# Denominators of linear attention inverted between two block transpositions, squares made by ScalarE, and a third buffer of key sums

## The chip, the cores and the metric

The kernel runs on one NeuronCore of a Trainium2 chip. The metric is the device time of one execution in microseconds. A NeuronCore has engines that run their own instruction queues side by side and wait for one another by semaphores: TensorE (PE in the profile, its weight loads PEld), VectorE (DVE), ScalarE (ACT), GpSimd (POOL) and SyncE (SP), which here issues the DMAs. Each engine executes its queue in order. Data lies in SBUF (128 partitions) or in PSUM, which has eight banks of 128 x 512 fp32 and takes what TensorE writes.

## The reference

Two images of 512 channels and 64 x 64 positions pass through four layers, each of the form x + layer(groupnorm(x)). The change concerns the fourth, an attention with random features (8 heads of 64 channels, 256 features):

```python
def _favor_softmax_features(data, proj, is_query):
    d = data.shape[-1]
    m = proj.shape[0]
    ratio = m ** (-0.5)
    normalizer = d ** (-0.25)
    data_dash = jnp.einsum('bhnd,md->bhnm', data * normalizer, proj)
    diag = 0.5 * jnp.sum((data * normalizer) ** 2, axis=-1, keepdims=True)
    if is_query:
        stab = jnp.max(data_dash, axis=-1, keepdims=True)
    else:
        stab = jnp.max(data_dash, axis=(-2, -1), keepdims=True)
    return ratio * (jnp.exp(data_dash - diag - stab) + EPS)
...
q = split_heads(t @ Wq)
k = split_heads(t @ Wk)
v = split_heads(t @ Wv)
qp = _favor_softmax_features(q, proj, is_query=True)
kp = _favor_softmax_features(k, proj, is_query=False)
context = jnp.einsum('bhnm,bhnd->bhmd', kp, v)
k_sum = jnp.sum(kp, axis=-2)
denom = jnp.einsum('bhnm,bhm->bhn', qp, k_sum)
out = jnp.einsum('bhnm,bhmd->bhnd', qp, context) / denom[..., None]
out = out.transpose(0, 2, 1, 3).reshape(B, N, C) @ Wo
```

Each token has one denominator a head.

## The kernel before

One image lies whole in SBUF as 4 chunks of 128 channels by 4096 positions (`X`, called `big0` or `big1` in the profile); the other image's space is lent out until the next image is loaded. A layer's work goes in 8 blocks of 512 positions (`blk`), and a block in 4 chunks of 128 channels, two heads each (`cc`). Matrix products are fp32; one product of 128 x 128 by 128 x 512 shows as two records of TensorE.

The fourth layer first goes over all blocks for the keys (`key_context`), which leaves the context `ctxm`, the key sums `ksum` and the small terms of EPS (`ends`). Then comes the stage of the queries, class `Queries`, `run` (L1800 on). For each block there are three generators, which `in_turn` steps one after the other until all are done:

- `prepare(blk)` (L1836), through `projected_squares` (L1544): for each chunk four matmuls make the query projection in a PSUM bank named `mm` (by `project`, L134), ScalarE copies it with its bias to `k` (L1554), and POOL squares it into `sq` (L1556).
- `score(blk)` (L1841): for each chunk, `features` multiplies `k` by the random projection in two halves and two heads (L1939, four `mm` banks) and ScalarE takes exponentials into `qf`, or into a lent part of an image, `big` (L1942). VectorE sums the squares (L1852) and takes the maxima over features (L1855) while it transposes 32 x 32 blocks. At the end of a block three small transposing matmuls (L1863) bring these together, ScalarE and VectorE make from them one factor for each token and head, `half`, which goes to DRAM (`lost`, L1873).
- `attend(blk)` (L1877): the factors come back from DRAM, repeated over 64 partitions for each head (`lost_all`, `fetch`, L1887). For each chunk POOL adds the two feature halves after weighing one by the ratio of the key sums (`qf_sum`, L1892 and L1894, for two heads); TensorE makes the numerator `psO` (L1906) and the denominator `psD` (L1910), the latter with the key sum repeated over 64 columns, so that all 64 partitions of a head hold the same row; VectorE adds the small term to the denominator (L1913), inverts it (L1914), adds the small term to the numerator (L1915) and multiplies the two into `k` (L1917). After four chunks the output projection follows (L1924), with the sum into `X` (L1927) and the store (L1928).

`attend(blk)`, `prepare(blk + 1)` (from block 1 to 6) and `score(blk + 1)` are stepped in turn, so a block's attention, the next block's features and the projection of the block after it are written interleaved. Block 0 has no projection beside it (that of block 1 was made with the first scores), the last block has neither. On top of that a scheduler reorders instructions within each engine's queue, by its own estimate of when they are ready; the orders named here are those of the compiled program.

PSUM has eight banks here: five for `mm` (shared by projections, features, score transpositions and output projections), two for `psO`, one for `psD`. `qf_sum` has two buffers, that is one chunk's pair; `lost_all` two; `sq` four. In the first three blocks the features of chunks 2 and 3 lie in the same lent place each time, so the next block's exponentials for it wait until the POOL sums have read it.

After the first image's stage, the second image's first layer begins: its weights are loaded into the space of the first image as that comes free, and its statistics are made within the last blocks (L965 to L978).

The parts that matter most, with their lines:

Of the kernel before, what the change touches and what calls it, by code (L numbers as in the profile page):

```python
# [9 lines left out]
F32 = mybir.dt.float32  # L10
I32 = mybir.dt.int32
AF = mybir.ActivationFunctionType
ALU = mybir.AluOpType
# [3 lines left out]
P = 128  # L17
# [4 lines left out]
TB = 512  # L22
# [20 lines left out]
def bcast(ap, axis, n):  # L43

    a = ap.unsqueeze(axis)
    shape = list(a.shape)
    shape[axis] = n
    return a.to_broadcast(shape)
# [10 lines left out]
class General:  # L59
# [130 lines left out]
    def layer0(self, X, Y, sp_scale, tokT, d):  # L190
        tc, nc, vec = self.tc, self.nc, self.vec
        with tc.tile_pool(name="l0", bufs=1) as sp:
# [7 lines left out]
            with tc.tile_pool(name="l0b", bufs=2) as wp, \  # L200
                    tc.tile_pool(name="l0s", bufs=2, space=PSUM) as pps, \
                    tc.tile_pool(name="l0m", bufs=3, space=PSUM) as pp, \
                    tc.tile_pool(name="l0o", bufs=1, space=PSUM) as ppo:
                taps = wp.tile([18, 9, P], F32, name="taps", bufs=1)
                nc.sync.dma_start(taps, d["taps"])
                steps = []
                for cc in range(KC):
                    steps += self.local_chunk(X, Y, cc, xs, nmean, rstd, sp_scale, tokT, taps, d,
                                              wp, pps, pp, ppo)
                in_turn(steps[0][0]())  # L210
                for i, (_, attend) in enumerate(steps):
                    ahead = [steps[i + 1][0]()] if i + 1 < len(steps) else []
                    in_turn(attend(), *ahead)
# [63 lines left out]
    def local_chunk(self, X, Y, cc, xs, nmean, rstd, sp_scale, tokT, taps, d, wp, pps, pp, ppo):  # L277
# [137 lines left out]
        def attend(blk):  # L415
# [48 lines left out]
            nc.vector.tensor_tensor(Y[:, cc, blk * TB:(blk + 1) * TB], acc, psO, ALU.add)  # L464

        return [(lambda b=b: prepare(b), lambda b=b: attend(b)) for b in range(NB)]


# [465 lines left out]
class Net(General):  # L934
# [606 lines left out]
                    queries.run(Y, dst, fp, pp, ppo, ppd, after_keys)  # L1541
        self.ahead.close()

    def projected_squares(self, X, w, bias, blk, out, sqs, wp, pp, made=()):  # L1544

        nc = self.nc
        for cc in range(KC):
            if made:
                ps = made[cc]
            else:  # L1550
                ps = pp.tile([P, TB], F32, name="mm")
                self.project(ps, w[:, :, cc * P:(cc + 1) * P], X, blk)
            k = out[:, cc, :]
            nc.scalar.activation(k, ps, AF.Identity, bias=bias[:, cc:cc + 1])  # L1554
            sq = wp.tile([P, TB], F32, name="sq", bufs=4)
            nc.gpsimd.tensor_tensor(sq, k, k, ALU.mult)  # L1556
            sqs.append(sq)
            yield

# [31 lines left out]
    def key_context(self, X, Y, d, queries, kp, wp, pp):  # L1591
# [54 lines left out]
        def contract(blk):  # L1646
            ks, ed, va = made.pop(blk)
            kf = {}
            for cc in range(KC):
# [31 lines left out]
                yield  # L1681

        in_turn(prepare(0))
        for blk in range(NB - 1):
            in_turn(contract(blk), prepare(blk + 1))
# [85 lines left out]
class Queries:  # L1771
# [64 lines left out]
    def prepare(self, blk, pp):  # L1836
        qs, sqs = self.wp.tile([P, KC, TB], F32, name="k"), []
        self.made[blk] = qs, sqs
        yield from self.net.projected_squares(self.X, self.wq, self.bq, blk, qs, sqs, self.wp, pp)

    def score(self, blk, fp, pp):  # L1841

        nc = self.nc
        qs, sqs = self.made.pop(blk)
        lost = self.yp.tile([2, KC, TB], F32, name="lost")
        fs = []
        self.scored[blk] = qs, lost, fs
        tops = fp.tile([P, 2, KC, 2, 16], F32, name="top_cols")
        sums = fp.tile([P, KC, 16], F32, name="sq_cols")
        for cc in range(KC):  # L1850
            fs.append(self.features(qs[:, cc], self.place(blk, cc, fp), pp))
            nc.vector.tensor_reduce(sums[:, cc], sqs[cc].rearrange("p (b i) -> p b i", i=32), AX.X,  # L1852
                                    ALU.add, apply_transpose=True)
            for h, f in enumerate(fs[cc]):
                nc.vector.tensor_reduce(tops[:, h, cc], f.rearrange("p j (b i) -> p j b i", i=32),  # L1855
                                        AX.X, ALU.max, apply_transpose=True)
            yield
        top = fp.tile([P, 2, KC, 16], F32, name="top_col")
        nc.vector.tensor_tensor(top, tops[:, :, :, 0], tops[:, :, :, 1], ALU.max)
        yield  # L1860
        ps = pp.tile([P, TB], F32, name="mm")
        for i, t in enumerate((sums, top[:, 0], top[:, 1])):
            nc.tensor.transpose(ps[:P // 2, i * P:(i + 1) * P], t.rearrange("p c b -> p (c b)"),  # L1863
                                self.net.ident)
        half = fp.tile([P // 2, 2, 32], F32, name="half")
        nc.vector.tensor_reduce(half, ps[:P // 2, :P].rearrange("p (h c i) -> p h i c", h=2, i=32),
                                AX.X, ALU.add)
        nc.scalar.activation(half, half, AF.Exp, scale=0.5 * HD ** -0.5)
        top = fp.tile([P // 2, 2, 32], F32, name="tops")
        nc.vector.tensor_reduce(top, ps[:P // 2, P:3 * P].rearrange(  # L1870
            "p (h c i) -> p h i c", h=2, i=32), AX.X, ALU.max)
        nc.vector.tensor_tensor(half, half, top, ALU.mult)
        nc.sync.dma_start(lost.rearrange("h c (b i) -> (c b) h i", i=32), half)  # L1873
        nc.vector.tensor_tensor(self.low, self.low, top, ALU.min)
        nc.vector.tensor_tensor(self.high, self.high, half, ALU.max)
        yield

    def attend(self, blk, ratio, dst, fp, pp, ppo, ppd):
        nc, X, ends, ctxm, ksum = self.nc, self.X, self.ends, self.ctxm, self.ksum
        qs, lost, fs = self.scored.pop(blk)  # L1880
        ends_of = {}

        def fetch(cc):

            ends_of[cc] = t = fp.tile([P, TB], F32, name="lost_all", bufs=2)
            for h in range(2):
                nc.sync.dma_start(t[h * HD:(h + 1) * HD, :], bcast(lost[h, cc], 0, HD))  # L1887

        def added(cc):
            ts = [fp.tile([P, TB], F32, name="qf_sum", bufs=2) for h in range(2)]  # L1890
            for h, t in enumerate(ts):
                nc.gpsimd.tensor_scalar(t, fs[cc][h][:, 1], ratio[:, 2 * cc + h:2 * cc + h + 1],  # L1892
                                        None, ALU.mult)
                nc.gpsimd.tensor_tensor(t, t, fs[cc][h][:, 0], ALU.add)  # L1894
            return ts

        for cc in range(2):
            fetch(cc)
        for cc in range(KC):
            sums = added(cc)  # L1900
            psD = ppd.tile([P, TB], F32, name="psD")
            psO = ppo.tile([P, TB], F32, name="psO")
            heads = [slice(h * HD, (h + 1) * HD) for h in range(2)]
            for j in range(2):
                for h, ch in enumerate(heads):
                    nc.tensor.matmul(psO[ch, :], ctxm[:, j, 2 * cc + h, :], fs[cc][h][:, j],  # L1906
                                     start=(j == 0), stop=(j == 1))
            for h, ch in enumerate(heads):
                g = 2 * cc + h
                nc.tensor.matmul(psD[ch, :], ksum[:, 0, g:g + 1].to_broadcast([P, HD]),  # L1910
                                 sums[h], start=True, stop=True)
            t = ends_of.pop(cc)
            nc.vector.scalar_tensor_tensor(psD, t, ends[:, 1, cc:cc + 1], psD, ALU.mult, ALU.add)  # L1913
            nc.vector.reciprocal(psD, psD)  # L1914
            nc.vector.scalar_tensor_tensor(t, t, ends[:, 0, cc:cc + 1], psO, ALU.mult, ALU.add)  # L1915

            nc.vector.tensor_tensor(qs[:, cc, :], t, psD, ALU.mult)  # L1917
            if cc + 2 < KC:
                fetch(cc + 2)
            yield  # L1920
        for oc in range(KC):
            ps = pp.tile([P, TB], F32, name="mm")
            for kc in range(KC):
                nc.tensor.matmul(ps, self.wo[:, kc, oc * P:(oc + 1) * P], qs[:, kc, :],  # L1924
                                 start=(kc == 0), stop=(kc == KC - 1))
            xx = X[:, oc, blk * TB:(blk + 1) * TB]
            nc.vector.tensor_tensor(xx, xx, ps, ALU.add)  # L1927
            nc.sync.dma_start(dst[:, oc, blk * TB:(blk + 1) * TB], xx)  # L1928
            yield
# [936 lines left out]
```

## Time and profile before

| what | value |
|---|---|
| median of 3 runs | 5015.74 us (5015.45 to 5020.18) |
| the profiled execution | 5015.88 us, its span 5014.0 us |
| mean granted TensorE clock | 0.984 |
| queries of the first image | about 2100 to 2522 us |
| queries of the second image | about 4588 us to the end |
| L1914, reciprocals | 64, 3362 ns each, 215.1 us |
| L1556, squares by POOL, median | 1.04 us |
| L1554, copy with bias by ScalarE | 0.69 us |

The page gives each engine's busy time over the whole span; the views by stretch, by waiting instruction and in order of time give the same for one stage. An idle time in brackets stands before the instruction that ends it, with the instruction that released it. Line numbers are those of the kernel before; the tail of a group such as `x64` is its count.

### The profile page before, as it was taken

Reading aid. Unit: us, or ns where it says so; the run is one execution under the profiler, and the core shown is the slowest. Engines: PE = TensorE matmul, PEld = TensorE weight load, DVE = VectorE, ACT = ScalarE, POOL = GpSimd, SP = SyncE. Lnnn points to the kernel's source line nnn. Section 1 sums busy time; section 2 is a strip of 40 time slices with the busy share of each in tenths; the row PEclk is TensorE's granted clock in tenths of the full one; section 3 lists DMA queues with packets and bytes.
Section 4 is the critical chain, followed back from the end, with each engine's and each line's share of the span. In section 5 each row is a group of like instructions: output and inputs, shape, how many; then the busy total and the mean of one; then the engine's idle time right before and its main releaser. Section 6 shows DMA issues by size and latency. Waiting matters only on the chain. (4 is left out here: it accounts for less than half of the span.)

```text
span 5014.0 us, 48290 instructions
## 1 busy us (share of the span) xinstructions
PE 4771.4 (95%) x16883; PEld 1971.8 (39%) x16883; DVE 3074.1 (61%) x3958; ACT 1816.8 (36%) x3477; POOL 1859.1 (37%) x1220
## 2 busy tenths in 40 slices
PE   7999998999999999999999999989999999999998
PEld 3433332554334444433343333335543344444333
DVE  4367776744679533477732777767446794335776
ACT  1256664244323233322112566642443242333221
POOL 0046665501320145554500466654014101554554
PEclk9999999999999999999999999999999999999999
DMA  3035555500000000211120455555000000000111
GB/s 154 1 103 155 155 156 164 160 19 10 1 17 0 1 1 1 72 55 44 58 74 2 126 154 157 151 159 150 12 10 1 17 1 1 1 1 24 43 45 43
DMA packets 129440, 313.29 MB, mean 62 GB/s; under 512 B 23394, under 2 KB 36194, under 8 KB 127652
## 3 DMA queue, kind: packets, MB, share of 16 engines
q1 hardware_dynamic: 129188, 310.12, 21.6%
q8 instruction: 135, 2.21, 0.2%
q14 instruction: 117, 0.96, 0.1%
HBM read 260.73 MB, written 49.31 MB: 62 GB/s over the span
## 5 line engine op out<-in xcount | busy, mean ns | idle before, releaser
L134 PE MATMUL mm<-big,w 128*128 128x512 f32 x2496 | 1164.9, 610 | 16.3 <-DVE big L2448 11.5
L134 PEld LDWEIGHTS mm<-big,w 128*128 128x128 f32 x2496 | 452.6, 191 | 698.3 <-issue 557.2
L2669 POOL TENSOR_TENSOR late<-late,big 128x1024 f32<-128x1024 f32 x194 | 458.5, 2363 | 223.4 <-DVE big L2664 185.4
L2489 DVE TENSOR_TENSOR prods<-qs,big 128x1024 f32<-128x1024 f32 (+1 forms) x200 | 332.2, 1686 | 60.1 <-PE tap L2527 49.1
L1669 POOL TENSOR_TENSOR big<-big 128x512 f32<-128x512 f32 x224 | 277.8, 1273 | 219.4 <-ACT big L1660 219.4
L2664 DVE TENSOR_TENSOR big<-big,mm 128x512 f32<-128x512 f32 x388 | 253.1, 681 | 114.9 <-ACT mm L2656 107.0
L1660 ACT ACTIVATE big<-mm,ed 128x256 f32<-128x256 f32 x512 | 193.5, 489 | 233.1 <-DVE top L1656 200.7
L2656 ACT COPY mm<-big 128x512 f32<-128x512 f32 x432 | 245.8, 597 | 60.4 <-DMA big<-rows 25.1
L2574 POOL TENSOR_TENSOR late<-late 128x512 f32<-128x512 f32 x84 | 105.3, 1275 | 410.5 <-ACT late L2559 393.9
L2669 POOL TENSOR_TENSOR late<-late,tap 128x1024 f32<-128x1024 f32 x94 | 222.1, 2363 | 94.5 <-DVE tap L2664 80.1
L1472 POOL TENSOR_TENSOR wq<-prob 128x512 f32<-128x512 f32 x48 | 71.6, 1515 | 487.9 <-ACT prob L1469 476.5
L1656 DVE TENSOR_REDUCE top<-mm 128x1 f32<-128x512 f32 x256 | 159.0, 684 | 148.1 <-PE mm L1587 148.1
L1924 PE MATMUL mm<-k,w 128*128 128x512 f32 x512 | 235.1, 602 | 12.4 <-DVE k L1917 7.5
L134 PE MATMUL mm<-big,wq 128*128 128x512 f32 x512 | 236.7, 608 | 2.7 <-ACT off_t L1243 2.7
L1215 PE MATMUL mm<-big,wo 128*128 128x512 f32 x512 | 238.1, 611 | 0.0
L1382 PE MATMUL acc<-big,diag 128*128 128x512 f32 x512 | 228.7, 604 | 9.8 <-ACT diag L1387 4.6
L1634 PE MATMUL mm<-w,big 128*128 128x512 f32 x512 | 234.5, 601 | 0.0
L973 POOL TENSOR_TENSOR group_stats<-group_stats,cst 128x1 f32<-128x1 f32 (+1 forms) x20 | 20.2, 1025 | 566.4 <-DVE group_stats L972 510.2
L2527 PE MATMUL tap<-prods,cst 128*32 128x512 f32 x1152 | 189.6, 620 | 29.2 <-ACT late L2538 26.5
L1914 DVE RECIPROCAL psD<-psD 128x512 f32<-128x512 f32 x64 | 215.1, 3362 | 1.9
L134 PE MATMUL mm<-big,big 128*128 128x512 f32 x464 | 201.7, 594 | 0.5 <-DVE b_sr L1011 0.5
L1469 ACT ACTIVATE prob<-mm 128x512 f32<-128x512 f32 x256 | 133.2, 603 | 171.4 <-PE mm L1466 171.1
(428 smaller groups left out, 8114.1 us busy)
## 6 DMA issues: line engine op xcount, KB each, us to landing
big<-rows SPq DMA_DIRECT2D x432, 256.0 KB
tap<-rows SPq DMA_DIRECT2D x208, 256.0 KB
yd<-late SPq DMA_DIRECT2D x32, 512.0 KB
lost_all<-lost SPq DMA_DIRECT2D x128, 128.0 KB
out<-big SPq DMA_DIRECT2D x64, 256.0 KB
big<-in_W_kv SPq DMA_DIRECT2D x8, 1024.0 KB
rows<-late SPq DMA_DIRECT2D x64, 128.0 KB
big<-in_x SPq DMA_DIRECT2D x32, 256.0 KB
```

The costliest lines, as they stand in the source:

```text
L134: self.nc.tensor.matmul(ps, w[:, kc, :], X[:, kc, blk * TB:(blk + 1) * TB], start=(kc == 0), stop=(kc == KC - 1))
L1215: nc.tensor.matmul(ps, w[:, kc, oc * P:(oc + 1) * P], att[:, kc, :], start=(kc == 0), stop=(kc == KC - 1))
L1382: nc.tensor.matmul(accs[b], dg, src[:, b * TB:(b + 1) * TB], start=(j == 0), stop=(j == 6))
L1634: nc.tensor.matmul(ps, X[:, kc, lo:lo + P], wv[:, kc, :], start=(kc == 0), stop=(kc == KC - 1))
L1660: nc.scalar.activation(f[:, t, :], pS[h][i][:, t % 2, :], AF.Exp, bias=ed[:, t, 2 * cc + h:2 * cc + h + 1])
L1669: nc.gpsimd.tensor_tensor(a, a, part, ALU.add)
L1914: nc.vector.reciprocal(psD, psD)
L1924: nc.tensor.matmul(ps, self.wo[:, kc, oc * P:(oc + 1) * P], qs[:, kc, :], start=(kc == 0), stop=(kc == KC - 1))
L2489: self.nc.vector.tensor_tensor(self.pair(u, k)[:, :n].rearrange("p k (y x) -> p k y x", x=W), bcast(qs.rearrange("p (y x) -> p y x", x=W), ...
L2656: nc.scalar.copy(ps, part)
L2664: nc.vector.tensor_tensor(part.rearrange("p (y x) -> p y x", x=W), self.vx[:, y:y + self.UY // 2, dx:dx + W], ps.rearrange("p (y x) -> p y ...
L2669: nc.gpsimd.tensor_tensor(out, out, t, ALU.add)
```

## The change

Three edits in the fourth layer's queries. For blocks 1 to 7 the squares are made by ScalarE, from the PSUM bank with the bias, instead of by POOL from the copy. `qf_sum` gets a third buffer; for the space, a small tile for maxima (`tops`, 64 x 64) is put into the tile of the squares' sums, `sq_cols`. The denominators, equal in the partitions of a head, are no longer inverted as 128 x 512: VectorE transposes each 32 x 32 block within the bank, inverts one column of each block (128 x 16), and transposes back while it repeats that column 32 times; the result goes to the second buffer of the chunk's key sums, whose matmul is done, and L1917 reads it there.

```diff
-    def projected_squares(self, X, w, bias, blk, out, sqs, wp, pp, made=()):
+    def projected_squares(self, X, w, bias, blk, out, sqs, wp, pp, made=(),
+                          by_act=False):
...
             nc.scalar.activation(k, ps, AF.Identity, bias=bias[:, cc:cc + 1])
             sq = wp.tile([P, TB], F32, name="sq", bufs=4)
-            nc.gpsimd.tensor_tensor(sq, k, k, ALU.mult)
+            if by_act:
+                nc.scalar.activation(sq, ps, AF.Square, bias=bias[:, cc:cc + 1])
+            else:
+                nc.gpsimd.tensor_tensor(sq, k, k, ALU.mult)
...
-        yield from self.net.projected_squares(self.X, self.wq, self.bq, blk, qs, sqs, self.wp, pp)
+        yield from self.net.projected_squares(self.X, self.wq, self.bq, blk, qs, sqs, self.wp, pp,
+                                                   by_act=blk > 0)
...
-        top = fp.tile([P // 2, 2, 32], F32, name="tops")
+        top = sums[:P // 2].rearrange("p c b -> p (c b)").rearrange("p (h i) -> p h i", h=2)
...
-            ts = [fp.tile([P, TB], F32, name="qf_sum", bufs=2) for h in range(2)]
+            ts = [fp.tile([P, TB], F32, name="qf_sum", bufs=3) for h in range(2)]
...
-            nc.vector.reciprocal(psD, psD)
+            nc.vector.transpose(psD, psD)
+            one = psD.rearrange("p (b r) -> p b r", r=32)[:, :, 0]
+            nc.vector.reciprocal(one, one)
+            nc.vector.transpose(sums[1].rearrange("p (b r) -> p b r", r=32), bcast(one, 2, 32))
             nc.vector.scalar_tensor_tensor(t, t, ends[:, 0, cc:cc + 1], psO, ALU.mult, ALU.add)
 
-            nc.vector.tensor_tensor(qs[:, cc, :], t, psD, ALU.mult)
+            nc.vector.tensor_tensor(qs[:, cc, :], t, sums[1], ALU.mult)
```

## The prediction

> **What bounds the kernel now.** I read the page's first part, then the times of TensorE's stretches in the stage that the change touches, then who releases TensorE there, then single instructions in order of time.
>
> ```profile
> PE 4771.4 (95%) x16883; PEld 1971.8 (39%) x16883; DVE 3074.1 (61%) x3958; ACT 1816.8 (36%) x3477; POOL 1859.1 (37%) x1220
> ...
> L1914 DVE RECIPROCAL psD<-psD 128x512 f32<-128x512 f32 x64 | 215.1, 3362 | 1.9
> ```
>
> TensorE is busy nearly throughout, so what the reciprocals cost VectorE (64 x 3.36 = 215 us) is not what can be won. Only TensorE's idle time can, so I asked for each engine's busy time in six stretches: first block, blocks 1 to 6 and last block of the fourth layer's queries, for each image. The columns are length, then busy time of PE, PEld, DVE, ACT, POOL, then granted clock, DMA share and GB/s.
>
> ```profile
> 2100.00:2175.00 75.00, 69.55 (x202) 24.84 (x199) 53.33 (x63) 20.43 (x38) 32.35 (x25) 0.93 0.13 44
> 2175.00:2475.00 300.00, 284.26 (x848) 100.89 (x847) 234.17 (x260) 68.09 (x127) 158.69 (x122) 1.00 0.16 55
> 2475.00:2525.00 50.00, 41.66 (x121) 16.79 (x120) 34.90 (x55) 0.81 (x4) 18.18 (x15) 1.00 0.44 152
> 4600.00:4650.00 50.00, 44.08 (x127) 15.23 (x125) 32.26 (x33) 15.16 (x28) 19.78 (x15) 0.90 0.07 22
> 4650.00:4970.00 320.00, 306.24 (x915) 109.86 (x916) 232.97 (x251) 68.35 (x128) 163.14 (x124) 1.00 0.13 43
> 4970.00:5014.00 44.00, 28.20 (x77) 9.68 (x73) 24.88 (x23) 0.00 (x0) 16.66 (x12) 0.86 0.16 55
> ```
>
> Length less PE: 5.5 + 15.7 + 8.3 us in the first image and 5.9 + 13.8 + 15.8 in the second, of which 6.7 lie after the last matmul (5007.3). So 58 us are idle. The clock takes more: 0.07 x 75 + 0.10 x 50 = 10 us in the two first blocks and up to 0.14 x 44 = 6 at the end. Some 74 us is the ceiling, and the other 4,200 us are untouched.
>
> Who holds TensorE shows in one chunk of a middle block, in the timeline (start, length, instruction, idle time before it and its releaser):
>
> ```profile
> 4837.28 3.37 DVE L1914 RECIPROCAL psD<-psD 128x512 f32<-128x512 f32 x1
> ...
> 4840.56 0.68 DVE L1915 SCALAR_TENSOR_TENSOR lost_all<-lost_all,ends,psO 128x512 f32<-128x512 f32 x1
> ...
> 4841.68 1.04 POOL L1556 TENSOR_TENSOR sq<-k 128x512 f32<-128x512 f32 x1
> ...
> 4842.75 0.71 DVE L1852 TRANSPOSE_TENSOR_REDUCE sq_cols<-sq 128x16 f32<-128x512 f32 x1 [1.52 <-POOL sq L1556]
> 4843.39 0.65 DVE L1917 TENSOR_TENSOR k<-lost_all,psD 128x512 f32<-128x512 f32 x1
> ...
> 4844.18 1.08 PE L1910 MATMUL psD<-qf_sum,ksum 128*64 128x512 f32 x4 [1.54 <-DVE k L1917]
> ```
>
> It is a ring. POOL's key sums (L1892 twice, 3.10 us, L1894 twice, 2.50) wait for the last psD matmul, since two buffers hold one chunk; the squares (1.04) come behind them in POOL's queue; VectorE's L1852 waits for the squares, with L1917 queued behind it; L1917 frees the one psD bank. Round trip: 1.08 + 3.10 + 2.50 + 1.04 + 0.71 + 0.65 = 9.1 us, nearly the 9.2 us from the psD matmul at 4835.01 to that at 4844.18. The reciprocal ends well before the squares do. In this block the three idle times before L1910 are 0.28 + 0.75 + 1.54 = 2.6 us.
>
> At the ends, where no projections cover it, VectorE's chain itself is what TensorE waits for:
>
> ```profile
> 4973.69 0.76 DVE L1913 SCALAR_TENSOR_TENSOR psD<-lost_all,ends,psD 128x512 f32<-128x512 f32 x1 [4.05 <-DMA lost_all<-lost]
> 4974.48 3.37 DVE L1914 RECIPROCAL psD<-psD 128x512 f32<-128x512 f32 x1
> ...
> 4978.57 1.08 PE L1906 MATMUL psO<-big,ctxm 128*64 128x512 f32 x1 [5.22 <-DVE lost_all L1915]
> ```
>
> [...] L1852, which transposes 512 fp32 columns as it reduces them, takes 0.70 us. [...] idle times of 3.25 us (to 2135.67) and 3.90 (to 4626.56) stand in the stretches with a granted 0.93 and 0.90. [...] No square stands between exponentials in this trace's query stage; the compiled order of the new kernel has as many table loads as the old (18, all branches), so I take no reload.
>
> **The change part by part.**
>
> Reciprocal. Removed: 3.36 us a chunk. Added: two transpositions and a reciprocal of 128x16. The transpositions are not in the trace in this form (fp32, in PSUM, and with a repeated source). Lower bound 0.55, a little under L1852; upper bound 1.3, twice it[...]; I take 0.70. The reciprocal: 64x64 takes 0.54 (4967), 512 columns 3.36, so 6.3 ns a column and 0.14 fixed: 0.24. In the compiled order L1915's work moves between the first transposition and the reciprocal, so it hides the wait between them. From the start of L1913's work to a free psD bank: 0.75 + 0.70 + 0.65 + 0.24 + 0.70, less overlaps of 0.1, = 2.9 us, where it was 0.76 + 3.37 + 0.67 + 0.65 = 5.4, and 7 with L1852's wait. The psO bank is free after 2.1, not 4.7. VectorE has room: 233 of 320 us before, less 24 x 1.7.
>
> Squares. 56 of 64 leave POOL (1.04 each) for ScalarE, from the bank, beside the copy with bias. Nearest row: L1554, 0.69 us; with L1428's squares at 0.73 the bounds are 0.6 and 0.73. ScalarE is busy 68 of 320 us, so 24 x 0.69 = 17 more fit. What waits: the projection's bank is held 0.69 us longer and the exponentials behind the square start up to 0.69 later. In the new order the next use of that bank is L1924's first matmul; before, L1554 ended at 4849.62 and L1924 began at 4850.74, so 0.69 fits with 0.4 to spare. Cost taken: nothing; if the cover is gone, up to 0.69 x 56 = 39 us, unlikely for each of them. L1852 no longer waits for POOL.
>
> Third buffer. The second sum of a chunk now keeps the inverted denominators until L1917, so three buffers carry one chunk and a half: one sum can be made ahead, the second waits for the last psD matmul and takes 1.55 + 1.25 = 2.8 us; where the first waits, both take 5.6. The new wait for L1917 of two chunks ago is long over in middle blocks. Sharing of the small tile for the maxima: same-engine order, nothing.
>
> Order. DMAs are as many as before and stand in nearly the same order on SP; the psD matmul of a block's second chunk moves ahead of a projection (3.7 us earlier), which spends some of the slack.
>
> **Sums.** *Middle blocks* (12): idle 15.7 + 13.8 = 29.5. With the ring cut, a chunk's chain (1.1 + 2.9, or 1.1 + 2.8 to 5.6 on POOL) is under TensorE's own 9 us. What is late next: the second chunk's psD matmul, which needs the first chunk's VectorE chain after `lost_all` landed. It landed 5.3 us after the block's first psO matmul (4821.21 against 4815.94); plus 2.9 is 8.2, and TensorE arrives after some 8.1 (two psO and two psD groups and a projection). I leave 0.4 us a block, 5 in all: gain 24.5.
>
> *First blocks.* `lost_all` lands at 2129.78 as before. Third psO matmul at 2131.9, not 2135.67; second psD matmul done at 2133.9; then POOL's 5.6 and 1.1 twice: fourth done at 2147.8. Before, it was issued about 2161.1. Remaining until L1863: two score and ten L1924 record pairs, about 9.8 us, so 2157.6 against 2158.73, with twelve more L1924 records (5.15) and one psD group (0.86) done: 7.1 us ahead. Twice: 14. The shorter stall may also spare half-clock time.
>
> *Last blocks.* Second image: third psO at 4975.9 instead of 4978.57; second psD matmul ends 4977.9; POOL gives the third chunk's sums at 4983.3 and the fourth's at 4988.9; its psD matmul ends at 4990; ten L1924 matmuls at 0.86 end at 4998.6, where they ended about 5006: 7. The first image's tail is followed by weight loads that POOL's last read of the image releases (2509.76, DMA at 2509.79); that read comes about 4.5 us earlier, the matmuls 7; I take 6.5.
>
> Total 24.5 + 14 + 13.5 = 52. The profiled execution took 5015.88 us (span 5014.0), 0.14 over the runs' median of 5015.74: 5015.88 - 52 = **4964 us**.
>
> **Rivals.** *Slow transpositions.* If they cost 1.3 each, a chain is 1.2 longer: 1.2 x 14 for the second chunks and 1.2 x 3 x 4 in first and last blocks, 31 us back: 4995. For it: no row shows this operation. Against: L1852's rate.
> *Banks held by squares.* TensorE waits 0.4 to 0.7 at half of the 56 squares: 11 to 20 us back, 4975 to 4984. For it: five banks for everything. Against: 21% busy ScalarE and the 0.4 to spare.
> *Slower than before.* [...] The chain is 6.3 us, over the old 5.4; above about 2.0 a transposition it is longer than the old one. The second chunk's psD matmul then waits 3.6 in each of 12 blocks, against 2.5 lost now, +13; first and last blocks gain nothing and lose 1 us a chunk, 3 x 4 = +12: 5041. Against it: L1852 again.
> *Nothing gained*, because the next stage absorbs it, could hide the first image's tail only.
>
> **How the numbers follow.** Forecast 0.75 (its own range 4948 to 4980), held banks 0.11, slow transpositions 0.08, slower 0.04, no change 0.02. The 8-in-10 range, widened for half-clock time spared (10 us more) and for the two milder rivals: 4944 to 4990. A measurement of this kernel tells about 0.2%, 10 us. Faster 0.94, within 0.02, slower 0.04.
>
> **What would show it.** Transpositions at 0.6 to 0.8 us and the small reciprocal near 0.24; TensorE idle in the middle stretches down from about 2.5 to under 0.8 a block; no wait of L1910 for POOL's squares; L1924's waits for ScalarE no larger; the half clock gone or shorter at the first blocks. Wrong if transpositions exceed 1 us, if TensorE's new idle time names ScalarE, or if the second chunk's psD matmul waits over 1 us.

## The result, and the profile after

The changed kernel takes 4940.91 us (median of 4 runs, 4936.16 to 4942.82), the kernel before beside it 5015.59. The ratio is 0.9848, 95% interval 0.9831 to 0.9865: 74.7 us less, where 52 were forecast. The direction was right; 4940.91 lies 3 us below the range's lower end of 4944.

First the engines' line of the page of the changed kernel, then the four new groups of instructions (after the bar: busy time, mean ns of one, and idle time of the engine before them):

```profile
PE 4742.3 (96%) x16883; PEld 1971.3 (40%) x16883; DVE 2987.0 (60%) x4086; ACT 1842.7 (37%) x3533; POOL 1813.3 (37%) x1164
```

```profile
L1919 DVE STREAM_TRANSPOSE psD<-psD 128x512 f32<-128x512 f32 x64 | 46.7, 730 | 2.1
L1922 DVE STREAM_TRANSPOSE qf_sum<-psD 128x512 f32<-128x512 f32 x64 | 45.4, 710 | 6.1 <-POOL qf_sum L1899 0.5
L1921 DVE RECIPROCAL psD<-psD 128x16 f32<-128x16 f32 x64 | 16.4, 257 | 0.0
L1558 ACT ACTIVATE sq<-mm,bq 128x512 f32<-128x512 f32 x56 | 38.0, 679 | 0.0
```

The same number of TensorE records is now "busy" for 29.1 us less (4771.4 before). That is the first sign that part of the gain was not in the idle time at all. The stretches of the query stage, in the columns of the table of before (length, busy PE, PEld, DVE, ACT, POOL, granted clock, DMA share, GB/s), with bounds that moved with the work:

```profile
2100.00:2175.00 75.00, 72.44 (x221) 26.20 (x222) 54.25 (x86) 23.31 (x44) 37.12 (x26) 1.00 0.17 61
2175.00:2448.00 273.00, 270.82 (x837) 101.38 (x836) 198.27 (x300) 78.15 (x149) 133.11 (x95) 1.00 0.17 57
2448.00:2490.00 42.00, 38.66 (x109) 15.09 (x108) 26.77 (x60) 0.80 (x4) 16.15 (x13) 0.96 0.45 147
4561.00:4611.00 50.00, 47.18 (x146) 16.49 (x145) 35.16 (x51) 16.52 (x31) 24.48 (x18) 1.00 0.12 31
4611.00:4900.00 289.00, 288.93 (x892) 107.70 (x890) 193.13 (x288) 79.59 (x151) 137.77 (x96) 1.00 0.13 46
4900.00:4941.00 41.00, 29.90 (x82) 10.66 (x81) 18.85 (x32) 0.00 (x0) 14.49 (x10) 0.87 0.19 60
```

In the second image's middle blocks TensorE is busy 288.93 of 289.00 us: nothing is left to win there while its own work stays the same. Both first blocks run at full clock, 1.00 (0.93 and 0.90 before, where 0.50, the "half clock" of these texts, was granted from 2135.60 to 2141.00 and from 4626.50 to 4629.00 us). Only the two last stretches stand lower (0.96 and 0.87).

One chunk of a middle block, in order of time (start, length, instruction, idle time before it and its releaser):

```profile
4762.10 0.76 DVE L1918 SCALAR_TENSOR_TENSOR psD<-lost_all,ends,psD 128x512 f32<-128x512 f32 x1 [4.28 <-DMA lost_all<-lost]
4762.90 0.73 DVE L1919 STREAM_TRANSPOSE psD<-psD 128x512 f32<-128x512 f32 x1
...
4763.53 0.71 DVE L1923 SCALAR_TENSOR_TENSOR lost_all<-lost_all,ends,psO 128x512 f32<-128x512 f32 x1
...
4764.16 0.26 DVE L1921 RECIPROCAL psD<-psD 128x16 f32<-128x16 f32 x1
4764.53 0.72 DVE L1922 STREAM_TRANSPOSE qf_sum<-psD 128x512 f32<-128x512 f32 x1
...
4765.39 1.08 PE L1915 MATMUL psD<-qf_sum,ksum 128*64 128x512 f32 x4
4765.76 0.65 DVE L1925 TENSOR_TENSOR k<-lost_all,qf_sum 128x512 f32<-128x512 f32 x1
...
4766.40 3.70 PE L134 MATMUL mm<-big,w 128*128 128x512 f32 x8
```

The chain from L1918's start to the free bank takes 3.15 us (4762.10 to 4765.25), and the view shows no idle time before the psD matmul of the block's second chunk. What frees the bank is now the second transposition (L1922). The product (L1925) no longer reads the bank, and L1857, the sum of the squares, stands behind the transposition too.

To see where the time went, I cut the stage at the score transpositions (L1863 before, L1868 after), which stand once at the end of each block's scores. "First two" is from block 0's to block 2's, "middle five" from there to block 7's. "Last block" is from there to the start of the next layer's first products in image 1 (L985), and to the start of the last output projection record in image 2.

| stretch | before, image 1 and 2 | after, image 1 and 2 | gain |
|---|---|---|---|
| first two blocks | 97.2, 98.0 us | 84.4, 84.8 us | 26.0 |
| middle five blocks | 262.1, 255.0 us | 243.3, 238.2 us | 35.6 |
| last block | 41.3, 40.7 us | 36.5, 36.2 us | 9.3 |
| the rest of the program | | | about 2 |

### The profile page after: what moved, and what is told of

It reads as the page before. It is cut to its first block, busy times and chain, and to the rows that moved or that the text cites. A ratio compares the mean times of both kernels' runs of the same rounds, so it can differ in the third digit from the quotient of the medians.

```text
span 4941.0 us, 48482 instructions
## 1 busy us (share of the span) xinstructions
PE 4742.3 (96%) x16883; PEld 1971.3 (40%) x16883; DVE 2987.0 (60%) x4086; ACT 1842.7 (37%) x3533; POOL 1813.3 (37%) x1164
## 5 line engine op out<-in xcount | busy, mean ns | idle before, releaser
L1932 PE MATMUL mm<-k,w 128*128 128x512 f32 x512 | 232.0, 600 | 0.8 <-DVE big L1935 0.8
L1897 POOL TENSOR_SCALAR qf_sum<-qf,ksum_ratio 128x512 f32<-128x512 f32 x64 | 100.4, 1570 | 265.4 <-PE psD L1915 212.6
```

## The experiments

The three edits make a cube of eight kernels. Of the six corners beside before and after, all were run, then four variants and the changed kernel once more. Blocks are read as in the table above, in one profiled execution of each kernel; times are medians, and each is set against the kernel before on the same chip. Line numbers in a run's views are those of that run's kernel; the names tell which instruction it is: `psD<-qf_sum,ksum` is the denominator's matmul, `k<-lost_all,...` the product that follows the inversion.

**Squares alone.** The kernel before with `by_act`:

```diff
-            nc.gpsimd.tensor_tensor(sq, k, k, ALU.mult)
+            if by_act:
+                nc.scalar.activation(sq, ps, AF.Square, bias=bias[:, cc:cc + 1])
+            else:
+                nc.gpsimd.tensor_tensor(sq, k, k, ALU.mult)
```

> The kernel before with only the squares on ScalarE. Ring theory (middle blocks lose time because a round of POOL's sums, POOL's squares and VectorE's L1852 and product frees the one psD bank every 9.1 us): without the 1.04 of the squares and the wait of L1852 for them the round is about 8 us, below TensorE's 9, so the middle blocks gain most of their 3.3 us each, 30 to 36 us over both images, while the first and last blocks gain next to nothing: 4980 to 4986. Chain theory (the length of the reciprocal is what costs, in the middle blocks too): under 10 us gained, 5006 or above.

Measured 5001.87 us, ratio 0.9966 (0.9954 to 0.9978), 17 us less. Middle blocks of the second image fall from 51.0 to 49.3 us (246.5 over five), half of the way to 47.6; the first two stay (97.0 and 99.2). Neither forecast was met. In one block the waits that are left (0.19 us at 4818.84, 0.76 here) name the product, which frees the bank:

```profile
4825.77 0.65 DVE L1922 TENSOR_TENSOR k<-lost_all,psD 128x512 f32<-128x512 f32 x1
...
4826.56 1.08 PE L1915 MATMUL psD<-qf_sum,ksum 128*64 128x512 f32 x4 [0.76 <-DVE k L1922]
```

So with the squares out of the way VectorE's own queue up to the product is next in line: the long reciprocal, which ends at 4824.12, then the numerator's sum and one of the maxima. The ring theory had part of the cause but gave this one cut too much.

**Third buffer alone.** The maxima go into `sq_cols` for the space, as in the changed kernel:

```diff
-            ts = [fp.tile([P, TB], F32, name="qf_sum", bufs=2) for h in range(2)]
+            ts = [fp.tile([P, TB], F32, name="qf_sum", bufs=3) for h in range(2)]
```

> The kernel before with only the third buffer of key sums. Ring theory: one of a chunk's two sums can be made ahead, so the round loses 2.8 of its 9.1 us and the middle blocks gain most of 3.3 us each, up to 36 us; the first and last blocks, where the wait is for VectorE's chain and then for POOL, gain a few us: about 4975 to 4990. If the squares in front of L1852 in VectorE's queue are what frees the bank late, and not the sums, it gains under 12 us: above 5003.

Measured 5008.40 us, ratio 0.9978 (0.9970 to 0.9987), 11 us less: the ring theory's 4975 to 4990 was missed, its alternative of under 12 us met. The middle blocks of the second image do not move (51.1 us). The profiled execution was the slowest of twelve (5013.64 us) and shows a gain only in the first two blocks (94.6 and 94.4 us for 97.2 and 98.0). TensorE's waits in the middle still name the squares and the product: in this run's timeline

```profile
4825.78 1.08 PE L1910 MATMUL psD<-qf_sum,ksum 128*64 128x512 f32 x4 [0.58 <-DVE k L1917]
...
4833.51 1.08 PE L1910 MATMUL psD<-qf_sum,ksum 128*64 128x512 f32 x4 [0.76 <-POOL sq L1556]
```

A sum made ahead doesn't help a bank that is freed late.

**Transposed inversion alone.** POOL squares, two buffers:

```diff
-            nc.vector.reciprocal(psD, psD)
+            nc.vector.transpose(psD, psD)
+            one = psD.rearrange("p (b r) -> p b r", r=32)[:, :, 0]
+            nc.vector.reciprocal(one, one)
+            nc.vector.transpose(sums[1].rearrange("p (b r) -> p b r", r=32), bcast(one, 2, 32))
...
-            nc.vector.tensor_tensor(qs[:, cc, :], t, psD, ALU.mult)
+            nc.vector.tensor_tensor(qs[:, cc, :], t, sums[1], ALU.mult)
```

> The kernel before with only the inversion between two transpositions; POOL still makes the squares and the key sums keep two buffers, of which the second now stays held until L1917. Chain theory: nearly all of the 75 us come from here, 4945 to 4955. Ring theory: the first two blocks of each image (26 us in all with the whole change) and the last ones (9) gain most of it, since there TensorE waits for VectorE's chain, but the middle blocks keep their round, and POOL waits longer for the second buffer: 4978 to 4992, no gain or a loss in the middle blocks.

Measured 5091.42 us, ratio 1.0143 (1.0128 to 1.0159): 72 us *slower*, and both theories had forecast a gain. Each inversion is shorter by 1.7 us, and middle blocks take 56.5 us. The waits of POOL show why (line waited for, releaser, us in total, times, longest). In the second image, before:

```profile
POOL qf_sum L1892 <- PE psD L1910: 170.8, 30, 18.1
```

and with the transposition alone:

```profile
POOL qf_sum L1892 <- PE psD L1910: 120.5, 15, 16.9
POOL qf_sum L1892 <- DVE k L1920: 54.7, 26, 4.0
```

POOL, which had waited only for TensorE (and at times for features), now waits for VectorE's product 26 times, since that product reads the buffer that POOL wants. A new arc goes from VectorE back to POOL.

**Squares and transposition, two buffers.** The changed kernel with `bufs=2` and its own tile for the maxima:

```diff
-            ts = [fp.tile([P, TB], F32, name="qf_sum", bufs=3) for h in range(2)]
+            ts = [fp.tile([P, TB], F32, name="qf_sum", bufs=2) for h in range(2)]
```

> The changed kernel with two buffers of key sums again: transposed inversion and ScalarE's squares alone. If it is mostly the squares that stretched the round of the transposition alone, the round is 1.1 + 3.9 (VectorE to the product) + 2.8 (POOL's second sum) = 7.8 us here, below TensorE's 9, and the time is 4945 to 4965. If it is the second buffer, held until the product, it stays slower than the kernel before: 5025 to 5080.

Measured 5071.52 us, ratio 1.0112 (1.0096 to 1.0127), within the forecast for the held buffer. The squares take back a quarter of the loss; the held buffer is most of it.

**Buffer and transposition, POOL squares.** The changed kernel with the old squares:

```diff
-            if by_act:
-                nc.scalar.activation(sq, ps, AF.Square, bias=bias[:, cc:cc + 1])
-            else:
-                nc.gpsimd.tensor_tensor(sq, k, k, ALU.mult)
+            nc.gpsimd.tensor_tensor(sq, k, k, ALU.mult)
```

> The changed kernel with the squares back on POOL: transposed inversion and third buffer alone. Ring theory: with the third buffer the round that made the transposition alone slower (psD matmul, VectorE's chain to the product, then POOL's second sum, 11 us) loses its last step, and the squares' 1.04 us on POOL still fit, since POOL then needs 5.6 + 1.04 + 1.1 = 7.7 us of TensorE's 9: middle blocks of 47.6 to 48.5 us, 4941 to 4955. Rival (squares in POOL's queue hold VectorE's product wherever they stand): middle blocks of 49 us and more, 4965 or above.

Measured 5002.57 us, ratio 0.9973 (0.9963 to 0.9984): the forecast missed by 50 us, the rival was right, and the reason can be read off one chunk of its timeline:

```profile
4877.17 1.56 POOL L1892 TENSOR_SCALAR qf_sum<-qf,ksum_ratio 128x512 f32<-128x512 f32 x1 [2.75 <-DVE k L1920]
...
4878.70 1.04 POOL L1556 TENSOR_TENSOR sq<-k 128x512 f32<-128x512 f32 x1
...
4879.77 0.71 DVE L1852 TRANSPOSE_TENSOR_REDUCE sq_cols<-sq 128x16 f32<-128x512 f32 x1 [2.80 <-POOL sq L1556]
...
4885.73 0.69 DVE L1920 TENSOR_TENSOR k<-lost_all,qf_sum 128x512 f32<-128x512 f32 x1
...
4886.62 1.57 POOL L1892 TENSOR_SCALAR qf_sum<-qf,ksum_ratio 128x512 f32<-128x512 f32 x1 [2.75 <-DVE k L1920]
```

POOL's sum waits for the product; the squares stand behind the sum in POOL's queue; L1852 waits for the squares; the product stands behind L1852, the maxima and the inversion in VectorE's queue. One round is 9.45 us (4877.17 to 4886.62), while TensorE needs 8.27 from psD matmul to psD matmul in the same chunk (4868.50 to 4876.77). A sum of busy times (7.7 of 9 us) cannot see this; only the two queues read together show it. TensorE pays for the lag at the end of the block, where an output projection (L1927) needs a bank that VectorE's late sum into `X` (L1930) frees. From 4800 to 4960 us (us in total, times, longest):

```profile
PE mm L1927 <- DVE big L1930: 9.9, 3, 3.3
```

With this wait of 3.3 us comes a lower clock as well (0.94 granted over each of the last three middle blocks).

**Squares and buffer, long reciprocal.**

```diff
-            nc.vector.transpose(psD, psD)
-            one = psD.rearrange("p (b r) -> p b r", r=32)[:, :, 0]
-            nc.vector.reciprocal(one, one)
-            nc.vector.transpose(sums[1].rearrange("p (b r) -> p b r", r=32), bcast(one, 2, 32))
+            nc.vector.reciprocal(psD, psD)
```

> The changed kernel with the long reciprocal again: ScalarE's squares and third buffer alone. Ring theory: the bank's round is 1.1 + 5.4 us and POOL's second sum is 2.8, so the middle blocks come near 48 us, while the first two blocks of each image stay near 95 us (85 in the changed kernel) with the half clock, and the last ones near 41: 4975 to 4990. Chain theory (the reciprocal counts everywhere): no better than the squares alone, 4998 or above.

Measured 4994.89 us, ratio 0.9950 (0.9937 to 0.9964), 22 us less, between the two theories. The middle blocks stand at 49.4, as with the squares alone; the first two at 94, as with the buffer alone. The two gains add up in the main (17 and 11, together 22); the rest of the 75 needs the other inversion.

**A tile of its own.** The inversion alone again, but the result goes to a new tile. In space it costs the same as the third buffer, and it too puts the maxima into `sq_cols`; `qf_sum` keeps two buffers and POOL the squares:

```diff
+            inv = fp.tile([P, TB], F32, name="inv", bufs=1)
-            nc.vector.transpose(sums[1].rearrange("p (b r) -> p b r", r=32), bcast(one, 2, 32))
+            nc.vector.transpose(inv.rearrange("p (b r) -> p b r", r=32), bcast(one, 2, 32))
...
-            nc.vector.tensor_tensor(qs[:, cc, :], t, sums[1], ALU.mult)
+            nc.vector.tensor_tensor(qs[:, cc, :], t, inv, ALU.mult)
```

> The kernel before with the transposed inversion, whose result goes to a tile of its own instead of the second key sum (the small tile for maxima shares the squares' sums, as in the changed kernel); two buffers of key sums, squares on POOL. It differs from the transposition alone only in which tile is held until the product. If that hold is what cost 75 us there, POOL's sums again wait for the psD matmul alone (1.1 + 5.6 + 1.04 = 7.7 us of 9) and the time is near the changed kernel's, 4941 to 4960. If the transposition itself delays VectorE, or if sums made ahead are needed, 5000 or above.

Measured 4947.33 us, ratio 0.9864 (0.9849 to 0.9879): 69 us less, with neither the ScalarE squares nor a third buffer. The same view of POOL's waits as above has no wait for VectorE's product any more:

```profile
POOL qf_sum L1892 <- PE psD L1910: 145.1, 23, 17.6
```

The new inversion is then nearly the whole gain, provided its result does not hold what POOL waits for; the ScalarE squares and the third buffer are one way to live with that hold. Middle blocks are 48.0 us, the first two 85.6 and 85.5. From a second chunk's psD matmul on (PEld loads its weights):

```profile
4816.49 0.19 PEld L1910 LDWEIGHTS psD<-qf_sum,ksum 128*64 128x64 f32 x2 [0.25 <-POOL qf_sum L1894]
...
4817.47 0.71 DVE L1852 TRANSPOSE_TENSOR_REDUCE sq_cols<-sq 128x16 f32<-128x512 f32 x1 [1.98 <-POOL sq L1556]
```

L1852 still waits for POOL's squares, now for 1.98 us, but the bank is free before it (the second transposition ends at 4815.49) and TensorE doesn't wait behind it. The edit does two things to the bank: the inversion is shorter, and its result leaves the bank, so the product need no longer come before the next psD matmul. A long reciprocal with its result in a tile of its own would tell the two apart; it was not run. With ScalarE's squares and three buffers a short chain is enough by itself: in the next experiment the product reads the bank, as with the long reciprocal above, and the middle blocks take 47.6 us instead of 49.4.

**Without the inversion.** The changed kernel without L1919 to L1922, L1925 multiplying by `psD`:

```diff
-            nc.vector.transpose(psD, psD)
-            one = psD.rearrange("p (b r) -> p b r", r=32)[:, :, 0]
-            nc.vector.reciprocal(one, one)
-            nc.vector.transpose(sums[1].rearrange("p (b r) -> p b r", r=32), bcast(one, 2, 32))
...
-            nc.vector.tensor_tensor(qs[:, cc, :], t, sums[1], ALU.mult)
+            nc.vector.tensor_tensor(qs[:, cc, :], t, psD, ALU.mult)
```

> The changed kernel without any inversion: the two transpositions and the small reciprocal are left out and the numerator is multiplied by the denominator, so the output is not divided. It shows what is left to win. If TensorE is at its floor in the middle blocks, the block stays at 47.55 to 47.8 us there, and only the first and last blocks gain, by up to 1.7 us a chunk: 4930 to 4939. If VectorE's chain still sets the pace in the middle blocks, these fall too, by 0.4 us or more each: under 4928.

Measured 4945.76 us, ratio 0.9855 (0.9840 to 0.9870), which overlaps the changed kernel's. Middle blocks 47.6 us in the second image: the floor. That the ends would gain was wrong; what is left of the inversion costs nothing that these runs can tell.

**Towards a better version.** The changed kernel once more, then the tile of its own with ScalarE's squares, then this with the second head's sum made by VectorE in the first and last block. The edit of the last one against the changed kernel, without the lines of the tile of its own, which are those above:

```diff
-            ts = [fp.tile([P, TB], F32, name="qf_sum", bufs=3) for h in range(2)]
+            ts = [fp.tile([P, TB], F32, name="qf_sum", bufs=2) for h in range(2)]
...
+                if h == 1 and blk in (0, NB - 1):
+                    nc.vector.scalar_tensor_tensor(t, fs[cc][h][:, 1], ratio[:, 2 * cc + h:2 * cc + h + 1],
+                                                   fs[cc][h][:, 0], ALU.mult, ALU.add)
+                    continue
```

> The changed kernel once more, on the same chip as the two versions below, so that a few tenths of a per cent can be compared: 4938 to 4944.

> The changed kernel with two buffers of key sums and a tile of its own for the inverted denominators, in the same space: the squares are on ScalarE. If the round through POOL and VectorE was the only loss, the middle blocks are at TensorE's floor already (47.6 us against 48.0 with the tile of its own and POOL's squares), and nothing but that 0.4 us a block comes off: 4938 to 4944, as the changed kernel. If POOL's sums, no longer waiting for VectorE's product, shorten the last blocks too: down to 4930.

> The kernel of own_squares where in the first and last block VectorE makes the second head's key sum in one instruction (about 0.75 us) instead of POOL in two (2.8 us). If POOL's 5.6 us a chunk and the half clock that follows the wait are what is left in the last blocks, the last two chunks come some 2.5 us earlier each and the two images gain 6 to 10 us together: 4930 to 4936. If the factors' way through DRAM (5.3 us) or the wait of VectorE's queue for them sets the end, nothing is gained, or a few us lost: 4938 to 4946.

Measured 4940.94 (ratio 0.9842, 0.9828 to 0.9855), 4944.58 (0.9852, 0.9837 to 0.9867) and 4938.04 us (0.9838, 0.9825 to 0.9851). With the tile of its own, the middle blocks stay at 48.1 us with ScalarE's squares too, so the 0.4 us against 47.6 doesn't come from POOL's squares. The traces show where it comes from. In each of the five middle blocks of the second image, and in all three kernels with a tile of its own, the second chunk's psD matmul waits for POOL's second sum, as in the lines above (L1894); with two buffers these sums are begun only after the first chunk's psD matmul. In the changed kernel, whose third buffer lets one sum be made ahead, this matmul doesn't wait for POOL.

The third version gains over the second: all five of its runs (4934.56 to 4941.30 us) lie below all four of the other (4942.16 to 4945.49), 6.5 us between the medians. In the profiles its last blocks are 4.2 and 3.2 us shorter (34.4 for 38.5 us and 34.2 for 37.4), though the mean granted clock of its profiled execution was lower (0.986 against 0.989). So POOL's 5.6 us a chunk did hold the last blocks, as the forecast of 6 to 10 us has it (its 4930 to 4936 had set out from the changed kernel's time). The longest wait remains: 3.17 us before the third psO matmul, whose releaser is the numerator's sum after the factors from DRAM. Against the changed kernel the 2.9 us are not told apart, since the runs overlap; what the ends win, the middle blocks lose for want of the third buffer. The changed kernel with VectorE's sums in the first and last blocks was not run. No version was found that is measurably faster than the changed kernel.

## Why the prediction was too cautious, point by point

The mechanism was right in the main: TensorE's waits at the psD bank and in the first and last blocks are what could be won, and the new operations cost what was taken. What failed are two terms of the sum, the middle blocks (24.5 us, for ten of twelve blocks 20.4 where 35.6 were measured) and the half clock at the first and last blocks (nothing, where the first gave up to 5 us an image). That the measured 74.7 us fall on the "ceiling" of 74 is chance: the middle blocks gave more than their whole idle time of 29.5, and the ends keep some of theirs.

*Costs of the new operations:* right. 0.73 and 0.71 for the transpositions (0.70 taken), 0.257 for the small reciprocal (0.24), 0.68 for the square (0.69), 3.15 for the chain (2.9). The two rivals with dear transpositions (1.3 us each, and a chain of 6.3; no trace had shown such lengths, they were the author's estimates) fell with the first row. ScalarE's squares held no bank that TensorE missed: before the output projections, L1932, stands 0.8 us of idle time in the whole program. They cost no reload either: ScalarE loads tables ten times in both traces.

*The ring in the middle blocks:* right in part. The cut by squares alone, by buffer alone and by both (middle blocks 49.3, 51.1, 49.4 us) shows that it needs the other inversion as well, and the tile of its own (48.0) that this alone nearly suffices, with POOL's squares where they were. What the prediction did not see is a second ring through POOL and VectorE that the changed buffer opens: 72 us slower alone, and closed only by the squares and the third buffer together, or by a tile of its own. The remark that "three buffers carry one chunk and a half" had found the held buffer but priced it at nothing, with no word on what it costs without the squares.

*Middle blocks, the first step that failed in size:* "idle 15.7 + 13.8 = 29.5", less "0.4 us a block". For the ten blocks measured here that makes 10 x 24.5 / 12 = 20.4 us; the gain was 35.6. The middle five blocks of the second image, before and then after:

```profile
4710.00:4965.00 255.00, 242.84 (x737) 86.83 (x736) 183.64 (x190) 56.31 (x105) 131.24 (x100) 1.00 0.13 42
```

```profile
4658.00:4896.00 238.00, 237.93 (x736) 88.72 (x735) 158.90 (x230) 66.11 (x125) 114.80 (x80) 1.00 0.13 45
```

736 or 737 records, at full clock both times, and "busy" for 4.9 us more in the kernel that waits. The idle time read was 12.2 us; what could be won, and was, is 16.8. I followed these blocks from the start of one TensorE record to the start of the next. Of the 16.8 us, 13.8 are waits at the psD matmuls, more than the view prints. In the block of the prediction's chunk the three steps to a psD matmul that waits take 0.87, 1.35 and 2.13 us. Undisturbed they take 0.52 after a projection (the first two) and 0.42 after psO: 2.9 us in excess, where the view prints 0.28, 0.75 and 1.54, 2.57 in all.

The other 3.0 us are no wait at all. Before, the psD matmuls of two chunks in each block cut a projection into six records and two:

```profile
4824.16 2.84 PE L134 MATMUL mm<-big,w 128*128 128x512 f32 x6
...
4828.29 1.13 PE L134 MATMUL mm<-big,w 128*128 128x512 f32 x2
```

After, the eight follow one another, in 3.70 us (4766.40 above). A step within a projection takes 0.43 us from start to start, one between different products mostly 0.52, and with what follows each cut costs 0.3; ten of them stand in these five blocks. The prediction saw that a psD matmul "moves ahead of a projection", but put nothing on it for TensorE. Of the 0.4 us a block that it took off, little came: two of the five blocks are 0.3 and 0.1 us longer than the other three (47.84 and 47.66 against 47.55). The chunk shown above is in the longest, where the psD matmul starts 8.36 us after the block's first psO matmul (4757.03 to 4765.39) and its bank was free after 8.22. How the first image's middle blocks divide was not worked out.

*First blocks, the second step that failed in size:* 14 us, with "the shorter stall may also spare half-clock time" left out of the sum, though the same text had read 10 us of it. First blocks and block 1 together gained 26.0, where the steps give 14 + 2 x 24.5 / 12 = 18.1. The cut by stretch (block 0's to block 2's score transposition, image 1, before and after):

```profile
2121.70:2218.90 97.20, 90.34 (x255) 31.41 (x254) 72.56 (x75) 21.43 (x39) 49.61 (x37) 0.95 0.11 39
```

```profile
2122.30:2206.70 84.40, 82.06 (x256) 29.20 (x255) 60.90 (x91) 23.31 (x44) 46.02 (x32) 1.00 0.13 44
```

Idle time fell by 4.5 us (6.9 to 2.3); the clock gave up to 0.05 x 97 = 4.9; the rest, 3.4, lies in "busy" and was not divided into waits and order of the products. Twice this is about the gain. The work part (9.0 an image) was a little too large, against 8.0 without the clock, although its sum has a slip that makes it half a microsecond too small (2133.9 and twice 5.6 + 1.1 is 2147.3, not 2147.8). The clock part was left at nothing. In the first image's first block TensorE waited 3.25 us before the third psO matmul, at 2135.67, and 0.50 was granted at the end of that wait and behind it:

```profile
2135.60:2141.00 5.40, 5.33 (x12) 1.43 (x12) 3.91 (x4) 0.00 (x0) 0.00 (x0) 0.50 0.15 52
```

In the second image the wait was 3.90 us, and 0.50 was granted in the 2.5 us behind it. After, these waits shrank to

```profile
2132.00 1.90 PE L1911 MATMUL psO<-big,ctxm 128*64 128x512 f32 x6 [1.75 <-DVE lost_all L1923]
...
4583.28 1.90 PE L1911 MATMUL psO<-big,ctxm 128*64 128x512 f32 x6 [2.23 <-DVE lost_all L1923]
```

and the clock stayed at 1.00 in both first blocks. A stall beside which the trace of before had 0.50 should have been put into the sum with both values of the clock.

*Last blocks:* 13.5 expected, 9.3 measured: 4.8 for 6.5 in the first image, 4.5 for 7 in the second. In the first image the last record of the output projections starts 6.1 us earlier (39.9 before, 33.8 after, from the last score transposition), but the next layer's products only 4.8. In the second the third psO matmul follows the factors from DRAM by 2.3 us, about as worked out (4905.22 to 4907.50), but TensorE still stands idle 3.01 us before it, and 6.8 us at half clock (0.50) come with it (4906.65 to 4913.48), as before (4977.67 to 4984.50). The second profile of the changed kernel (the first of the three kernels under "Towards a better version") has 2.77 us there and no half clock until after the last matmul: its last block takes 33.8 us instead of 36.2. So the half clock is worth about 2 us here, most of what was missing; in the same program it came in one profile and stayed away in the other. The sum had left it out at this place too.

The sum of the differences: 35.6 - 20.4 = 15.2 in the middle, 7.9 at the start, -4.2 at the end, and 2 in the rest of the program: 21, which is 73 (the two profiled spans) less 52.

## What to carry to other kernels

Judge a loss by the time between two repeats of the same instruction, against the pace of an undisturbed repeat, not by the idle time that a view prints: here the same 736 or 737 records showed 4.9 us more of busy time in the kernel whose matmuls waited. Then take out what the order of the queue alone changes: each projection cut in two by a psD matmul cost 0.3 us here without any wait. When a result is put into a buffer that another engine fills, write down the whole round through both queues, with what stands ahead of each instruction: an edit that shortens every operation can be slower, and a separate tile for the same space can be worth more than another buffer of the shared one. And price a stall beside which a trace shows half clock (here after waits of 3.01, 3.25 and 3.90 us) twice, with and without it: in the last block of the changed kernel it made about 2 us.

## What the runs showed of the hardware

The half clock did not come with every wait of about the same length. In the kernel with buffer and transposition alone, three middle blocks of the second image with the same longest wait (3.3 us by the view) had a clock of 1.00, 1.00 and 0.97, and the next three 0.94. In the last block of the changed kernel a wait of 3.01 us was followed by 0.50 in one profile (4907.50 to 4913.00 us), and one of 2.77 in the other was not.

Where VectorE's product reads both operands from SBUF, most of those that ran beside a two-operand instruction of POOL took longer. In the changed kernel the product (L1925) reads both operands from SBUF. Of the 21 that ran beside such an instruction (for at least 0.05 us), 16 took over 0.8 us, up to 1.81, where those with none beside them took 0.65 to 0.69; with the tile of its own (POOL squares) it is 41 of 47, up to 1.83. At 4769.69 us such a product took 1.80 us, and the second of the two POOL sums beside it 1.72, where 1.27 is usual. In the kernel before, one operand of the product lies in PSUM, and none of 22 beside such instructions took more than 0.69; nor did any of 49 in the four other runs whose product reads PSUM (squares alone, buffer alone, squares and buffer, no inversion). No run was made for this alone. The psD bank doesn't wait for these products; whether they cost time elsewhere was not separated.
